# Two graph layers, one instruction order: a sum moves ahead of the output's statistics, the output's scaling moves back, and the first two periods are reordered

## The chip, the cores and the metric

The kernel runs on one core of a Trainium2 chip. Its time is the device time of one execution in microseconds (us); the figure given is the median of three runs. Five engines work side by side, each through its own list of instructions in order: TensorE (PE in the profile) multiplies, VectorE (DVE), ScalarE (ACT) and GpSimd (POOL) do the elementwise work, SyncE (SP) issues the transfers. They wait for each other through semaphores.

## The reference

There are 128 graphs of 128 nodes with 512 features. Each passes through two layers. The first is an attention over neighbours with 8 heads, the second a hypergraph convolution with a hidden width of 1024. Each layer is added to its input and normalized over the features.

```python
feats = einsum('bnf,hfu->bhnu', X, W)
dense = leaky_relu(e_self[..., :, None] + e_neigh[..., None, :], 0.2)
att   = softmax(dense + NEG_BIG * (1 - A), axis=-1)
x     = layernorm(x + relu(einsum('bhij,bhju->bhiu', att, feats) + b))

conv(x, W, b) = Dn * (H @ (Be * (H.T @ (x @ W.T)))) + b      # H = (adj != 0)
h     = layer_norm(relu(conv(x, W1, b1)), gamma, beta)
x     = layernorm(x + (conv(h, W2, b2) + x))
```

All of it is in fp32. A and H are the same 0/1 matrix of a graph, and H H^T with its two scalings is one 128 x 128 matrix, R in the kernel.

## The kernel before, in words

**Pairs.** Two graphs (g = 0, 1) make a pair, so there are 64 pairs (p). The three large products of a pair (features pf with W, hidden ph with W1, output weights py with W2) are each made as a 2 x 2 block product by seven smaller products instead of eight. The function `chain` lays down one such set. Its products go to three PSUM banks, called X, Y and W: 1 to X, 2 to Y, 6 onto X, 5 to W, 7 onto X, 4 onto X, 3 onto W, in this order. X is copied out by ACT (L343) after product 1, after product 6 and after product 7, and PE may add the next product to X only after that copy. The four quarters of the result are then sums of two pieces. For the hidden values h these sums are `h_sum` (L865, on DVE); `relu` (L880, on ACT) follows each of them. `h_sum(g, q)` makes quarter q of graph g; the one in question is `h_sum(1, 0)`, which needs products 1 and 6 and, last, 5 and 3 (bank W). For the features the sums are `f_sum` (L508 on DVE, one quarter on ACT). The sums of operands that the seven products need are made ahead: for the inputs xS, zS and hS on POOL, for the weights once at the start (`prepare_hidden` for W1, L248; `prepare_output_blocks` and `prepare_output_block_sums` for W2, L299 and L225).

**The order is written out by hand.** Each operation of a pair is registered with `at(lag, time, ...)` or `@step(lag, time)`: a lag in periods and a time within a period of T = 38.6. Its key is time + (p + lag) * T. All operations of all pairs are sorted by their keys once and emitted in this order, and each engine runs its own share in that order. The keys are places in a row, not real times. So in one period of the steady state the kernel works on several pairs at once: loads and masks of pair p, features of p - 1, attention of p - 2, hidden layer of p - 3, output of p - 4. The table `first` overrides keys for the first pairs, and `todo` holds the work done once, with keys of its own; there the first full period begins at 115.8.

**PE's order in a period**: `propagate` (pz, R times the first layer's output y), `propagator` (pd, makes R for a later pair), ph products 1, 2, 6, 5, 7, `output` (pq, R times y2), ph products 4 and 3, pf products 1, 2, 6, 5, 7, py product 1, pf products 4 and 3, the attention `attend_pair` (pav), py products 6, 2, 7, 5, 4, 3.

**DVE's order around the change**: `o_sum` for both graphs (L1023, adds the output to the skip path), `o_stats` for both (bn_stats L758 and bn_aggr L759), the variance column of `rstds` (L764), `h_sum(1, 0)` (L865), the transposes eT of graph 0's attention (L639), `o_norm` (L769, scales the output), `f_sum` twice (L508), eT of graph 1, the last `f_sum`, and `spread_rows` (rows, L541).

**POOL**: the power of `rstds` (L766 gives rso for the output and rsa for the first layer), `squares` (L903, sums squares of h in three levels for each graph), `h_sums` (hS, L468), then the mask of a pair (neg, L377), rsa, `masked` (L588, adds the mask to the neighbour scores nb), zS (L839), and others.

**ACT**: copies of X (L343), relu, the squares of h (L891), the first layer's output (L793), zT (`z_evict`, L828: pz out of PSUM), `leaky` (L604) and `exponential` (L618) on nb. `largest` (L610, on DVE) stands between these two.

**Transfers.** All go through SP's queue in the order of the keys: e_write and e_read (ed, eb: the attention scores to DRAM and back), `load_blocks` (xb), `store` (L1041, 512 KB of output), `load_edges` (ab), then rows are written to DRAM (rd, L551) and read back spread over all partitions as nb (L569, two transfers of 512 KB). `load` brings a (adjacency) and w; w has one buffer, which `nodes` (L359 to L368) reads.

Of the kernel before, what the change touches and what calls it, by code (L numbers as in the profile page):

```python
# [20 lines left out]
def kernel(  # L21
# [45 lines left out]
    nc = tc.nc  # L67
# [244 lines left out]
    LAST = PAIRS - 1  # L312
    steps = []

    def step(lag, time, since=0, until=PAIRS):

        def keep(fn):
            steps.append((lag, time, fn.__name__, range(since, until), fn, ()))
            return fn
        return keep  # L320

    def at(lag, time, fn, *args, since=0, until=PAIRS):
        steps.append((lag, time, fn.__name__, range(since, until), fn, args))
# [444 lines left out]
    def normalize(s, key, t, g):  # L768
        nc.vector.tensor_scalar(  # L769
            t, t, s["mv", key][:, g, 0:1], s["rs", key][:, g:g + 1], op0=ALU.subtract,  # L770
            op1=ALU.mult,
        )
# [95 lines left out]

    at(3, 5.9, h_sum, 0, 0, 0, "Y")
    at(3, 10.75, h_sum, 1, 1, 2, "W")  # L870
    at(3, 16.4, h_sum, 1, 0, 1, "W")

    def relu(p, s, g, q):
        dst = hid(s, g, q)
# [44 lines left out]
    def weigh(s, i, to, start):  # L919
# [3 lines left out]
          QU, 1, until=LAST)  # L923
# [105 lines left out]
    at(4, 13.3, o_sum, 1, until=LAST)  # L1029
    at(4, 14.7, o_stats, 0, until=LAST)  # L1030
    at(4, 15.5, o_stats, 1, until=LAST)
    at(4, 15.6, rstds, "o", until=LAST)

    @step(4, 17.0, until=LAST)
    def o_norm(p, s):
        for g in range(2):
            normalize(s, "o", s["o"][:, g, :], g)

    @step(4, 19.5, until=LAST)
    def store(p, s):  # L1040
        nc.sync.dma_start(out[2 * p:2 * p + 2].rearrange("g n f -> n g f"), s["o"])  # L1041

# [79 lines left out]
    for t, fn, *args in (  # L1122
# [20 lines left out]
        (12.95, load_first_row, (1,)),  # L1143
        (15.46, load_weights, (nc.sync, w1_blocks[:1:-1], w1t, F // 2, HALF)),
        (16.1, everywhere, (b2_bc, b2, nc.sync)),
        (79.0, prepare_hidden, (nc.gpsimd, 2)), (79.1, prepare_hidden, (nc.gpsimd, 0)),
        (98.0, prepare_hidden, (nc.gpsimd, 1)), (110.6, prepare_hidden, (nc.vector, 3)),
        (15.5, prepare_output_vectors, ()), (16.0, prepare_output, ()),
        (78.3, prepare_rows, ()), (78.79, prepare_output_sums, ()),
        (78.99, prepare_output_spread, (0, "gw")), (98.0, prepare_output_spread, (1, "bw")),  # L1150
# [2 lines left out]
        (117.8, prepare_output_blocks, (slice(2, 3),)),  # L1153
        (118.1, prepare_output_blocks, (slice(3, 4),)),
        (126.5, prepare_output_block_sums, (nc.gpsimd, slice(0, 2))),
        (127.7, prepare_output_block_sums, (nc.vector, slice(2, 3))),
        (134.5, prepare_output_block_sums, (nc.vector, slice(3, 4))),
        (100.0, prepare_mean_columns, ()),
    ]

# [5 lines left out]
        ("r_evict", 0): 97.845,  # L1166
        ("spread_rows", 1): 15.72, ("nodes", 1): 15.55, ("write_nodes", 1): 15.85,
        ("edges", 1): 110.4, ("scale_edges", 1): 110.5, ("neighbours", 1): 80.1,
        ("propagator", 1): 117.76, ("spread_nodes", 1): 80.3, ("r_evict", 1): 121.8,
        ("leaky", 0, 1, 1): 77.65, ("leaky", 0, 0, 1): 73.6, ("largest", 0, 0, 1): 75.3,  # L1170
        ("attend", 0, 0, 0): 78.95, ("attend", 0, 0, 1): 78.96, ("attend", 0, 1, 0): 78.97,
        ("attend", 0, 1, 1): 78.98, ("attended", 0, 0): 97.8, ("attended", 0, 1): 97.82,
        ("add_bias", 0, 0): 13.6, ("add_bias", 0, 1): 13.61,
        ("residual", 0, 0): 97.81, ("residual", 0, 1): 97.83, ("rstds", 0, "a"): 97.84,
        ("leaky", 1, 0, 0): 117.85, ("leaky", 1, 0, 1): 117.9, ("leaky", 1, 1, 0): 119.9,
        ("largest", 1, 0, 0): 118.0, ("largest", 1, 0, 1): 118.2, ("largest", 1, 1, 0): 120.2,
        ("masked", 1, 0, 0): 109.0, ("masked", 1, 1, 1): 121.5,
        ("nodes", 2): 142.2, ("write_nodes", 2): 143.0, ("nodes", 3): 150.0,
        ("write_nodes", 3): 150.1, ("skip", 0): 132.5,
    }  # L1180

    def run(fn, p, args):
# [87 lines left out]
```

## Time and profile before

| | |
|---|---|
| time, median of 3 runs | 2442.08 us (2441.72 to 2445.27) |
| span of the profiled execution | 2440.8 us |
| PE busy | 2369.9 us (97%) |
| DVE busy | 2000.1 us (82%) |
| POOL busy | 1816.2 us (74%) |
| ACT busy | 1524.7 us (62%) |
| DMA, mean rate | 142 GB/s |

The span is that of one traced execution. Busy time is the time in which an engine has at least one instruction under way; for PE the ends are modelled. A line of a timeline gives start, duration, engine, line of the kernel, operation, what is written and read, shapes and how often in a row; in brackets stands the engine's idle time just before and what ended it. A line of waits gives who waited for whom: total us, how often, the longest. The core ran at a mean granted clock of 0.998.

### The profile page before, as it was taken

What the parts mean: (1) busy time and instruction counts of PE and PEld (TensorE: products, weight loads), DVE (VectorE), ACT (ScalarE), POOL (GpSimd) and SP (SyncE); (2) the same over time, 40 slices, a digit from 0 to 9 for tenths busy, and PEclk for the clock granted to TensorE, in tenths of its full rate; (3) what the DMA queues carried; (4) which work ended last, traced back from release to release, by engine and by line L of the source; (5) the groups of instructions that cost most, each with busy time, mean ns of one, the idle gap of its engine ahead of it and who ended that gap; (6) DMA issues with size and microseconds to landing.
All of it is one profiled execution on the core that took longest, in us unless ns stands there. A gap on an engine that the chain in (4) does not pass through costs nothing.

```text
span 2440.8 us, 81033 instructions
## 1 busy us (share of the span) xinstructions
PE 2369.9 (97%) x32309; PEld 2009.1 (82%) x32309; DVE 2000.1 (82%) x4456; ACT 1524.7 (62%) x4481; POOL 1816.2 (74%) x2060
## 2 busy tenths in 40 slices
PE   7999999999999999999999999999999999999998
PEld 5788888888888888888888888888888888888886
DVE  7888878888887888888888888887887888888876
ACT  4665756756656657557666566575576665665663
POOL 5777777777777777777777777777777777777774
PEclk9999999999999999999999999999999999999999
DMA  6545455545555455454445554544554555545441
GB/s 185 139 132 154 141 137 145 150 142 145 147 145 147 133 151 146 137 148 145 141 147 146 145 147 137 149 145 141 148 146 138 147 145 146 147 135 154 140 122 53
DMA packets 432872, 347.10 MB, mean 142 GB/s; under 512 B 153176, under 2 KB 382064, under 8 KB 432496
## 3 DMA queue, kind: packets, MB, share of 16 engines
q1 hardware_dynamic: 429024, 337.46, 48.4%
q8 instruction: 255, 4.18, 0.7%
q10 hardware_dynamic: 3472, 4.47, 0.6%
q14 instruction: 121, 0.99, 0.1%
HBM read 239.08 MB, written 102.73 MB: 140 GB/s over the span
## 4 chain that ended last, share of the span: by engine, by line
PE 83%; DVE 6%; ACT 5%; DMA 2%; issue 2%; POOL 1%; SPq 0%; ACTq 0%; POOLq 0%; DVEq 0%
PE pyX L97 17%; PE phX L97 16%; PE pyW L97 8%; PE phW L97 7%; PE pfX L97 7%; PE phY L97 4%; PE pav L702 4%; PE pz L97 4%; PE pyY L97 4%; PE pq L97 4%; ACT h L880 3%; PE pfW L97 2%; DVE h L865 2%; PE pfY L97 2%; PE pd L97 1%
## 5 line engine op out<-in xcount | busy, mean ns | idle before, releaser
L343 ACT COPY py<-pyX 128x257 f32<-128x257 f32 x189 | 70.9, 375 | 511.0 <-PE pyX L97 511.0
L97 PEld LDWEIGHTS phX<-zS,w_sb 128*64 128x64 f32 x6144 | 350.3, 137 | 38.1 <-POOL ft L741 23.1
L97 PE MATMUL phX<-zS,w_sb 128*64 128x128 f32 x6144 | 373.0, 273 | 4.3 <-POOL xS L468 2.2
L903 POOL TENSOR_TENSOR sq<-sq 128x512 f32<-128x512 f32 (+2 forms) x384 | 349.6, 911 | 20.1
L588 POOL TENSOR_TENSOR nb<-nb,neg 128x512 f32<-128x512 f32 x256 | 319.6, 1281 | 37.6 <-DMA nb<-rd 37.1
L604 ACT ACTIVATE nb<-nb,ft 128x128 f32<-128x128 f32 x1020 | 325.3, 392 | 19.2 <-POOL nb L588 17.3
L618 ACT ACTIVATE nb<-nb,nm 128x128 f32<-128x128 f32 x1024 | 319.1, 391 | 4.0 <-DVE nm L610 4.0
L880 ACT ACTIVATE h<-h,vecs 128x128 f32<-128x128 f32 x768 | 239.5, 393 | 76.7 <-DVE h L865 76.4
L766 POOL TENSOR_TENSOR rso<-veo,mhalf 128x2 f32<-128x2 f32 x63 | 44.2, 702 | 292.5 <-DVE veo L764 292.5
L97 PE MATMUL pyX<-w_sb,hS 128*64 128x257 f32 x2016 | 243.7, 379 | 0.5 <-POOL hS L468 0.5
L97 PE MATMUL pyX<-w_sb,h 128*64 128x257 f32 x2016 | 243.5, 379 | 0.5 <-ACT py L343 0.5
L97 PE MATMUL pyW<-w_sb,hS 128*64 128x256 f32 x2016 | 242.9, 378 | 0.4 <-DVE y L934 0.4
L97 PEld LDWEIGHTS pyX<-w_sb,h 128*64 128x64 f32 x2016 | 172.1, 136 | 47.7 <-ACT py L343 0.9
L97 PEld LDWEIGHTS pyW<-w_sb,hS 128*64 128x64 f32 x2016 | 171.5, 136 | 47.2 <-POOL neg L377 0.8
L741 POOL TENSOR_TENSOR ft<-ft,b_bc 128x512 f32<-128x512 f32 x128 | 203.9, 1613 | 6.4 <-ACT ft L532 6.4
L610 DVE TENSOR_REDUCE nm<-nb 128x4 f32<-128x512 f32 x256 | 175.3, 685 | 34.1 <-ACT nb L604 32.2
L97 PEld LDWEIGHTS pyX<-w_sb,hS 128*64 128x64 f32 x2016 | 165.5, 137 | 41.1 <-POOL hS L468 0.7
L97 PE MATMUL pfX<-w_sb,xS 128*64 128x264 f32 x992 | 136.2, 390 | 40.3 <-ACT pf L343 40.1
L639 DVE STREAM_TRANSPOSE eT<-eb 128x512 f32<-128x512 f32 x252 | 163.5, 687 | 0.0
L1006 DVE SCALAR_TENSOR_TENSOR y<-y,rsh,bw_bc 128x512 f32<-128x512 f32 x126 | 150.5, 1233 | 14.3 <-POOL rsh L1002 14.3
L804 DVE SCALAR_TENSOR_TENSOR o<-y,b_bc 128x512 f32<-128x512 f32 x128 | 162.1, 1305 | 0.0
L891 ACT ACTIVATE sq<-h 128x512 f32<-128x512 f32 x256 | 160.8, 629 | 2.1
(178 smaller groups left out, 5567.9 us busy)
## 6 DMA issues: line engine op xcount, KB each, us to landing
nb<-rd SPq DMA_DIRECT2D x127, 512.0 KB
ed<-nb SPq DMA_DIRECT2D x126, 512.0 KB
eb<-ed SPq DMA_DIRECT2D x504, 128.0 KB
x<-in_x_dram SPq DMA_DIRECT2D x64, 512.0 KB
out_dram<-o SPq DMA_DIRECT2D x63, 512.0 KB
xb<-in_x_dram SPq DMA_DIRECT2D x248, 128.0 KB
a<-in_adj_dram SPq DMA_DIRECT2D x64, 128.0 KB
w<-in_adj_dram SPq DMA_DIRECT2D x128, 64.0 KB
```

The lines of the kernel that those rows point to most:

```text
L97: nc.tensor.matmul(to[rows], lhs[:, rows], rhs, start=start, stop=stop, skip_group_check=True)
L588: nc.gpsimd.tensor_tensor(t, t, neg[:, :, None, :].to_broadcast([P, NB, HH, B]), op=ALU.add)
L604: nc.scalar.activation(t, t, AF.Prelu, bias=s["ft"][:, g, h, 0:1], alpha=SLOPE)
L610: nc.vector.tensor_reduce(s["nm"][:, g, hs], scores(p, s, g, hs).rearrange("p b h j -> p h b j"), AX.XY, ALU.max, negate=True,)
L618: nc.scalar.activation(t, t, AF.Exp, bias=s["nm"][:, g, h:h + 1])
L639: nc.vector.transpose(s["eT"][:, g, hs, :].rearrange("p h (b i) -> p h b i", b=NB), s["eb", g][:, :, hs, :].rearrange("p b h j -> p h b j"),)
L741: nc.gpsimd.tensor_tensor(t, t, b0_bc.rearrange("p (h u) -> p h u", h=H), op=ALU.add)
L804: nc.vector.scalar_tensor_tensor(s["o"][:, g, :], s["y"][:, g, :], 2.0, b2_bc, op0=ALU.mult, op1=ALU.add)
L880: nc.scalar.activation(dst[:, k, :], src[:, k, :], AF.Relu, bias=b1_sb[:, c:c + 1])
L891: nc.scalar.activation(s["sq"][:, g, q * KH // 2:(q + 1) * KH // 2, :], hid(s, g, q), AF.Square, scale=DH ** -0.5,)
L903: nc.gpsimd.tensor_tensor(t[:, :n, :], t[:, :n, :], t[:, n:2 * n, :], op=ALU.add)
L1006: nc.vector.scalar_tensor_tensor(t, t, s["rs", "h"][:, g:g + 1], bw_bc.rearrange("p (j c) -> p j c", j=2), op0=ALU.mult, op1=ALU.add,)
```

## The change

No instruction is added or taken away; keys change. It is meant to let each engine reach sooner what PE needs next.

In the steady state, `h_sum(1, 0)` goes ahead of the output's statistics in DVE's order (key 14.6, between `o_sum` at 13.3 and `o_stats` at 14.7). The columns for the output's scale are made later (17.3), behind `squares` of graph 0 on POOL and behind eT of graph 0 on DVE. `o_norm` moves behind eT of graph 1 (23.0), and the store behind `load_blocks` and `load_edges`, right ahead of the write of rows (24.3).

In the first two periods, the sums of W1 are made in the order in which the products use them; `masked`, `leaky` and `largest` of pair 1 come earlier, `propagator` of pair 1 later; two exponentials of pair 1 go behind the copies of X that stood behind them; `prepare_output_block_sums` on DVE, `squares` of pair 0 and `nodes` of pairs 2 and 3 with their transfers go later.

```diff
-    at(3, 16.4, h_sum, 1, 0, 1, "W")
+    at(3, 14.6, h_sum, 1, 0, 1, "W")
...
-    at(4, 15.6, rstds, "o", until=LAST)
-
-    @step(4, 17.0, until=LAST)
+    at(4, 17.3, rstds, "o", until=LAST)
+
+    @step(4, 23.0, until=LAST)
     def o_norm(p, s):
...
-    @step(4, 19.5, until=LAST)
+    @step(4, 24.3, until=LAST)
     def store(p, s):
...
-        (79.0, prepare_hidden, (nc.gpsimd, 2)), (79.1, prepare_hidden, (nc.gpsimd, 0)),
-        (98.0, prepare_hidden, (nc.gpsimd, 1)), (110.6, prepare_hidden, (nc.vector, 3)),
+        (79.0, prepare_hidden, (nc.gpsimd, 0)), (79.1, prepare_hidden, (nc.gpsimd, 1)),
+        (120.7, prepare_hidden, (nc.gpsimd, 2)), (110.6, prepare_hidden, (nc.vector, 3)),
...
-        (127.7, prepare_output_block_sums, (nc.vector, slice(2, 3))),
-        (134.5, prepare_output_block_sums, (nc.vector, slice(3, 4))),
+        (137.5, prepare_output_block_sums, (nc.vector, slice(2, 3))),
+        (141.0, prepare_output_block_sums, (nc.vector, slice(3, 4))),
...
-        ("propagator", 1): 117.76, ("spread_nodes", 1): 80.3, ("r_evict", 1): 121.8,
+        ("propagator", 1): 121.7, ("spread_nodes", 1): 80.3, ("r_evict", 1): 121.8,
...
-        ("leaky", 1, 0, 0): 117.85, ("leaky", 1, 0, 1): 117.9, ("leaky", 1, 1, 0): 119.9,
-        ("largest", 1, 0, 0): 118.0, ("largest", 1, 0, 1): 118.2, ("largest", 1, 1, 0): 120.2,
-        ("masked", 1, 0, 0): 109.0, ("masked", 1, 1, 1): 121.5,
-        ("nodes", 2): 142.2, ("write_nodes", 2): 143.0, ("nodes", 3): 150.0,
-        ("write_nodes", 3): 150.1, ("skip", 0): 132.5,
+        ("leaky", 1, 0, 0): 113.0, ("leaky", 1, 0, 1): 117.9, ("leaky", 1, 1, 0): 119.9,
+        ("largest", 1, 0, 0): 110.55, ("largest", 1, 0, 1): 118.2, ("largest", 1, 1, 0): 120.2,
+        ("masked", 1, 0, 0): 98.0, ("masked", 1, 0, 1): 98.1, ("masked", 1, 1, 0): 98.2, ("masked", 1, 1, 1): 121.5,
+        ("exponential", 1, 0, 0): 119.85, ("exponential", 1, 1, 1): 126.6,
+        ("squares", 0, 0, 0): 141.3, ("squares", 0, 0, 1): 141.4, ("squares", 0, 0, 2): 141.5,
+        ("nodes", 2): 144.2, ("write_nodes", 2): 144.3, ("spread_nodes", 2): 145.5,
+        ("nodes", 3): 154.6, ("write_nodes", 3): 154.7, ("skip", 0): 132.5,
```

## The prediction

> **What bounds the kernel now.** I read the page's busy times first: TensorE (PE) is the only engine near its limit.
>
> ```profile
> PE 2369.9 (97%) x32309; PEld 2009.1 (82%) x32309; DVE 2000.1 (82%) x4456; ACT 1524.7 (62%) x4481; POOL 1816.2 (74%) x2060
> ```
>
> So only a change of PE's own pauses counts. The list of PE's waits is second: one recurring line carries nearly all of it, the rest is the start.
>
> ```profile
> PE pfX L97 <- ACT pf L343: 40.1, 60, 1.0
> PE px L396 <- DMA x<-in_x_dram: 8.7, 1, 8.7
> ```
>
> Third, the timeline of one period, engine by engine. PE: after product 5 (pfW), product 7 (pfX) waits for ScalarE's (ACT's) copy of product 6 out of the same bank.
>
> ```profile
> 1009.56 1.09 PE L97 MATMUL pfX<-w_sb,xS 128*64 128x264 f32 x8
> 1010.45 1.09 PE L97 MATMUL pfW<-w_sb,xS 128*64 128x264 f32 x8
> 1012.17 1.11 PE L97 MATMUL pfX<-w_sb,xS 128*64 128x264 f32 x8 [0.64 <-ACT pf L343]
> 1013.08 1.94 PE L97 MATMUL pyX<-w_sb,h 128*64 128x257 f32 x16
> ```
>
> ACT: that copy stands behind the relu of h's second graph, first half (L880), which waits 1.21 for VectorE (DVE).
>
> ```profile
> 1008.90 0.38 ACT L343 COPY pf<-pfX 128x264 f32<-128x264 f32 x1 [0.48 <-PE pfX L97]
> 1010.48 1.28 ACT L880 ACTIVATE h<-h,vecs 128x128 f32<-128x128 f32 x4 [1.21 <-DVE h L865]
> 1011.67 0.36 ACT L343 COPY pf<-pfX 128x264 f32<-128x264 f32 x1
> ```
>
> DVE: the sum that relu needs (L865) stands behind both output statistics.
>
> ```profile
> 1006.80 1.24 DVE L1023 TENSOR_TENSOR o<-o,pq 128x512 f32<-128x512 f32 x2
> 1007.96 0.68 DVE L758 BATCH_NORM_STATS2 statso<-o 128x6 f32<-128x512 f32 x1
> ...
> 1009.69 0.17 DVE L764 TENSOR_SCALAR veo<-mvo 128x2 f32<-128x2 f32 x1
> 1009.77 0.68 DVE L865 TENSOR_TENSOR h<-ph,phW 128x512 f32<-128x512 f32 x1
> ...
> 1011.59 1.45 DVE L769 TENSOR_SCALAR o<-o,mvo,rso 128x512 f32<-128x512 f32 x2
> ...
> 1016.83 0.43 DVE L508 TENSOR_TENSOR ft<-pf,pfW 128x264 f32<-128x264 f32 x1 [1.46 <-PE pfW L97]
> ```
>
> A control exists: in the last period with pf products DVE has no "nodes" work, its sum comes 1.2 us earlier, and PE does not pause.
>
> ```profile
> 2350.83 1.09 PE L97 MATMUL pfX<-w_sb,xS 128*64 128x264 f32 x8
> 2351.72 1.09 PE L97 MATMUL pfW<-w_sb,xS 128*64 128x264 f32 x8
> 2352.61 1.09 PE L97 MATMUL pfX<-w_sb,xS 128*64 128x264 f32 x8
> ```
>
> **What the Trainium skill says.** "PSUM — Partial Sum Buffer", section "Engine vs sequencer instructions": the queues of ScalarE, VectorE and GpSimd are strict FIFO. The trace agrees: the copy at 1011.67 had its data from 1010.65 and went only after the relu. "Perfetto Trace Analysis", section "Tensor Engine Instruction (MATMUL, LD_WEIGHTS)": a matmul's end is modelled, so I count start to start: 1.72 from pfW to pfX here, 0.89 in the control; the pause costs 0.83, not 0.64. "DMA: Bandwidth & Descriptors", section "Queues, rings and completion order": each DMA engine takes the descriptors of one ring in ring order. That matters for the moved store, and no run here yet shows a small write directly behind it.
>
> **The change part by part.**
>
> *h_sum(1,0) to 14.6.* It moves between o_sum and o_stats; no instruction is added. Its input phW (started 1006.03, 1.94 long) ends at 1007.97, when DVE finishes o_sum (1008.04), so the new wait in front of the statistics is under 0.1. Sum 1008.0 to 1008.7; the relu follows ACT's first copy at 1009.2, ends 1010.4; product 6 is ready at 1010.65, its copy runs to 1011.03, product 7 may start at its natural 1011.34. Slack 0.3. The gain is 0.83, plus 0.02 at the next product, which starts 0.91 instead of 0.89 later. The periods agree: pz to pz is 37.24 in the steady state (1028.87 to 1066.11) and 36.37 in the control (2332.92 to 2369.29), 0.87 apart. Between 0.85 and 0.87 I take 0.86: 60 x 0.86 = 51.6.
>
> *o_stats, rstds, o_norm, store.* Behind the statistics on DVE stand eT, the pf sums and rows; they keep their order but for o_norm. DVE's new order from 1008.7: statistics 1.73, eT 1.22, veo 0.08, pf sum 0.35; then the pf sum that waits for product 7's copy (1011.34 + 1.56 = 1012.90), 0.34; eT 1.22; o_norm 1.37; end 1015.85. The next pf sum is ready at 1016.83 - 0.86 = 1015.97. o_norm fits into the old idle time of 1.46, with 0.1 to spare, and costs nothing. On GpSimd (POOL) the power for rso now stands behind the squares of graph 0, which need no DVE, so hS starts about 0.8 earlier than now: hidden.
>
> *The store* is the risk. Now:
>
> ```profile
> 1013.07 0.41 SPq L1041 DMA_DIRECT2D out_dram<-o  x1
> 1013.52 3.00 SPq L137 DMA_DIRECT2D ab<-in_adj_dram  x4
> 1017.64 0.34 SPq L551 DMA_DIRECT2D rd<-rows  x1
> 1019.08 1.51 SPq L569 DMA_DIRECT2D nb<-rd  x2
> ```
>
> New: o_norm's end 1015.9, store issued then, rd issued at 1017.64 - 0.86 = 1016.8. The 512 KB store now moves about 0.9 to 2.5 after issue (DMA is busiest from 1014 to 1015.5), so until about 1018.4; rd's write would land at 1018.2 and lands 0.65 later if it queues (0 if it does not, 1.5 if the store is slow). Then nb, masked on POOL, leaky on ACT, zT, phX are 0.65 late against PE. How much is free? POOL waited 2.61 for nb at 280.43, ACT then 2.00, and PE lost 0.81: PE loses what POOL's wait has over 1.8. POOL's usual wait is 37.1 / 39 = 0.95, so 0.85 is free. Only periods that are already late lose: three before. I allow 2.0 in all.
>
> *The first two periods.* The keys only change order; each instruction stays. Three edits follow one thought: POOL makes the weights' sums in the order of the products (0 and 1 early, 2 only ahead of product 7), masked, leaky and largest of pair 1 go ahead into ACT's and POOL's idle time before pz (ACT waits 1.36 there at 50.15, a leaky group takes 1.28), and no exponential stands ahead of a copy that PE needs. PE's pauses between 48 and 101 now: the propagator ahead of product 1 (phX starts 53.76 though zT is there at 50.74), 1.8 for ph's first copy behind an exponential that waits for DVE, 2.2 at 66.83 for the third copy behind the last exponential, 1.4 at 97.22. New: product 1 at 51.9, the first copy at 53.9 without the wait, product 6 at 55.3, propagator behind it. Then DVE, which is busy without a gap from 46 to 65 and does the same work, holds PE: its last block of prepare_output_blocks frees the bank of phW at 58.9, largest gives the exponential ahead of the second copy at 59.6, so product 7 is at 61.4 (now 62.72), product 4 at 64.4 (now 66.83), pfX at 67.9 (now 70.34). In the pf stretch the block sums move off DVE's path to f_sum and the squares behind hS on POOL, so rows leave near 77.5 (now 80.26). pz(1) then waits for a(3), which is loaded behind nb: rsa about 2.5 to 3 earlier than 91.33. Gain kept: 3.0, bounds 0 (the wait for a is unmoved) and 5.
>
> Sum: 2442.1 - 51.6 - 3.0 + 2.0 = 2389.5.
>
> **The rivals.**
>
> *The store takes the place of the copy.* If rd is 2.0 late instead of 0.65, each of the 39 periods in which POOL waits loses 0.95 + 2.0 - 1.8 = 1.15: 45 in place of the 2.0 allowed, so about 2432. For it: rd, nb, masked is a chain of 8 us with 0.85 free. Against: rd is only 16 KB and the store 512 KB, over in 1.5 us.
>
> *A rest of the wait stays.* If DVE reaches the sum 0.5 later than worked out (TENSOR_SCALAR beside a busy POOL varies: deg took 1.18 at 1028.09 where two columns elsewhere take 0.17), the copy is 0.25 late: 60 x 0.25 = 15, about 2405.
>
> *Slower.* The sum blocks DVE, and rows and rd come late with the store ahead: nb 2.4 later costs 0.95 + 2.4 - 1.8 = 1.55 in 39 periods, 60 in all, so about 2447. Against: phW ends before DVE is free, and the control shows 36.37 is reachable.
>
> **How the numbers follow.** Forecast 0.74, a rest of the wait 0.12, the store 0.09, slower or no gain 0.05. The time is the forecast's, 2389.5. Low 2382: no loss at nb, 5 at the start, and the three old pauses of zT (1.2) gone. High 2408: the rest of the wait. Faster by over 0.2% 0.94, same 0.03, slower 0.03.
>
> **What would show it.** Right: PE's line for pfX on pf gone, pfW to pfX 0.89, pz to pz near 36.4, sum L865 ahead of L758, o_norm ending within 0.2 of the last pf sum's start. The start: pz of pair 1 near 90.5 (now 93.44). Store: nb issued 2.1 to 2.8 after rd instead of 1.44, POOL's wait for nb grown from 37.1 to some 70. Wrong: a large PE line phX on zT or pq on y, a period above 36.8, or o_norm holding the last pf sum and rows.

## The result, and the profile after

The changed kernel takes 2464.82 us (median of 4 runs, 2460.85 to 2468.28) against 2442.34 of the kernel before (2441.72 to 2445.27; a fourth run stands beside the three above): ratio 1.0089 (1.0070 to 1.0108). It is 0.9% slower. The forecast was 2389.5, faster by 52.7; it was wrong, and the rival that forecast a slower kernel came nearest.

First the busy times, then the engines of the chain that ended last, on the page of the changed kernel; the last line is the chain of the kernel before:

```profile
PE 2378.2 (96%) x32309; PEld 1899.6 (77%) x32309; DVE 2040.1 (83%) x4456; ACT 1527.6 (62%) x4481; POOL 1807.7 (73%) x2060
...
PE 37%; DMA 28%; DVE 14%; POOL 8%; ACT 7%; SPq 3%; issue 3%; DVEq 0%; ACTq 0%; POOLq 0%
```

```profile
PE 83%; DVE 6%; ACT 5%; DMA 2%; issue 2%; POOL 1%; SPq 0%; ACTq 0%; POOLq 0%; DVEq 0%
```

PE is still the busiest engine, but it makes up only 37% of the chain, 83% before. 28% is DMA, 2% before. The list of PE's waits (who waited for whom: total us, times, longest) names the new wait:

```profile
PE phX L97 <- ACT zT L828: 53.7, 48, 2.6
PE px L396 <- DMA x<-in_x_dram: 8.0, 1, 8.0
PE pyW L97 <- DVE y L934: 5.0, 8, 1.0
PE pyX L97 <- POOL hS L468: 4.2, 2, 2.8
```

The line for pfX on pf, 40.1 before, is gone. In its place stands phX on zT. The list of all waits shows where that comes from (the last line shown is the first one's in the kernel before; there the second had 17.3 in 17 waits, and SP's wait for rd 79.4):

```profile
POOL nb L588 <- DMA nb<-rd: 129.5, 67, 6.2
...
ACT nb L604 <- POOL nb L588: 83.5, 55, 8.0
```

```profile
SPq L569 <- DMA rd<-rows: 163.0, 63, 4.1
```

```profile
POOL nb L588 <- DMA nb<-rd: 37.1, 39, 5.3
```

So nb comes late, POOL's masked is late, ACT's leaky is late, and zT stands behind leaky on ACT. The wait is there at the transfer rd already.

Start to start, PE's excess over the shortest time of each pair of products, summed from pair 1's pz on, makes the balance. Before: pfW to pfX 51.9, all else 7.1. After: pfW to pfX 0.2; pd to phX 61.5; phX and phY that run slowly after such a pause 9.6; pyX to pyW 6.0; pav to pyX 3.3; all else 3.6. That is 25 more, and 1.1 gained ahead of it (pz of pair 1 starts at 92.30 instead of 93.44). The last pair's pz starts 24.2 later than before (2424.83 against 2400.67).

One period of the changed kernel, DVE first:

```profile
1660.59 1.24 DVE L1023 TENSOR_TENSOR o<-o,pq 128x512 f32<-128x512 f32 x2
1661.75 0.68 DVE L865 TENSOR_TENSOR h<-ph,phW 128x512 f32<-128x512 f32 x1
1662.35 0.69 DVE L758 BATCH_NORM_STATS2 statso<-o 128x6 f32<-128x512 f32 x1
...
1666.83 1.30 DVE L639 STREAM_TRANSPOSE eT<-eb 128x512 f32<-128x512 f32 x2
1668.06 2.31 DVE L769 TENSOR_SCALAR o<-o,mvo,rso 128x512 f32<-128x512 f32 x2
1670.29 0.41 DVE L508 TENSOR_TENSOR ft<-pf,pfW 128x264 f32<-128x264 f32 x1
1670.81 0.24 DVE L541 STREAM_TRANSPOSE rows<-ft 128x32 f32<-128x32 f32 x1
```

The sum L865 follows o_sum at once, as predicted. But o_norm takes 2.31 for its two instructions, not 1.45, and the last pf sum, whose bank PE finished at about 1669.5, starts only at 1670.29. POOL at that time makes hS:

```profile
1666.15 2.51 POOL L468 TENSOR_TENSOR hS<-h 128x512 f32<-128x512 f32 x2
1668.74 1.34 POOL L468 TENSOR_TENSOR hS<-hS,h 128x512 f32<-128x512 f32 x1
1670.16 1.35 POOL L468 TENSOR_TENSOR hS<-h,hS 128x512 f32<-128x512 f32 x1
...
1679.82 4.98 POOL L588 TENSOR_TENSOR nb<-nb,neg 128x512 f32<-128x512 f32 x4 [1.69 <-DMA nb<-rd]
```

SP's queue, in this period and in an earlier one:

```profile
652.39 0.41 SPq L1041 DMA_DIRECT2D out_dram<-o  x1
653.07 0.34 SPq L551 DMA_DIRECT2D rd<-rows  x1
657.36 0.92 SPq L569 DMA_DIRECT2D nb<-rd  x2
...
1670.39 0.41 SPq L1041 DMA_DIRECT2D out_dram<-o  x1
1671.07 0.34 SPq L551 DMA_DIRECT2D rd<-rows  x1
1673.45 0.93 SPq L569 DMA_DIRECT2D nb<-rd  x2
```

From rd to nb it was 1.44 before. Here it is 2.38, and in the earlier period 4.29. Both periods have the store directly ahead of rd.

### The profile page after: what moved, and what is told of

Its sections match the earlier page's. It is cut to its first block, busy times and chain, and to the rows that moved or that the text cites. A ratio compares the mean times of both kernels' runs of the same rounds, so it can differ in the third digit from the quotient of the medians.

```text
span 2464.9 us, 81039 instructions
## 1 busy us (share of the span) xinstructions
PE 2378.2 (96%) x32309; PEld 1899.6 (77%) x32309; DVE 2040.1 (83%) x4456; ACT 1527.6 (62%) x4481; POOL 1807.7 (73%) x2060
## 4 chain that ended last, share of the span: by engine, by line
PE 37%; DMA 28%; DVE 14%; POOL 8%; ACT 7%; SPq 3%; issue 3%; DVEq 0%; ACTq 0%; POOLq 0%
PE phX L97 12%; DMA nb<-rd 11%; DMA rd<-rows 6%; PE phW L97 6%; DMA ed<-nb 5%; DVE o L769 5%; PE pfX L97 5%; ACT nb L604 4%; POOL nb L588 3%; PE phY L97 3%; DVE eT L639 3%; PE pq L97 3%; DMA eb<-ed 3%; PE pyX L97 2%; DMA sd<-sr 2%
## 5 line engine op out<-in xcount | busy, mean ns | idle before, releaser
L903 POOL TENSOR_TENSOR sq<-sq 128x512 f32<-128x512 f32 (+2 forms) x384 | 317.8, 828 | 215.4 <-ACT sq L891 195.3
L97 PEld LDWEIGHTS phX<-zS,w_sb 128*64 128x64 f32 x6144 | 344.9, 137 | 38.9 <-POOL ft L741 15.6
L97 PEld LDWEIGHTS pyW<-w_sb,hS 128*64 128x64 f32 x2016 | 149.2, 136 | 75.8 <-issue 6.8
L97 PEld LDWEIGHTS pyX<-w_sb,h 128*64 128x64 f32 x2016 | 149.3, 137 | 70.6 <-ACT py L343 0.9
L741 POOL TENSOR_TENSOR ft<-ft,b_bc 128x512 f32<-128x512 f32 x128 | 194.9, 1542 | 5.0 <-ACT ft L532 5.0
L97 PEld LDWEIGHTS pyX<-w_sb,hS 128*64 128x64 f32 x2016 | 144.6, 137 | 64.5 <-POOL hS L468 4.5
L97 PE MATMUL phX<-zT,w_sb 128*64 128x128 f32 x2048 | 131.0, 283 | 54.1 <-ACT zT L828 53.7
L639 DVE STREAM_TRANSPOSE eT<-eb 128x512 f32<-128x512 f32 x252 | 164.2, 690 | 13.4 <-DMA eb<-ed 13.3
L766 POOL TENSOR_TENSOR rsa<-vea,mhalf 128x2 f32<-128x2 f32 x64 | 44.8, 700 | 173.7 <-DVE vea L764 173.7
L97 PEld LDWEIGHTS phX<-zT,w_sb 128*64 128x64 f32 x2048 | 115.4, 141 | 67.5 <-ACT zT L828 67.1
L468 POOL TENSOR_TENSOR hS<-h 128x512 f32<-128x512 f32 x126 | 159.6, 1287 | 4.7 <-DVE w_sb L225 4.7
```

The costliest lines, as they stand in the source:

```text
L97: nc.tensor.matmul(to[rows], lhs[:, rows], rhs, start=start, stop=stop, skip_group_check=True)
L468: engine.tensor_tensor(t[:, i], in0, in1, op=op)
L639: nc.vector.transpose(s["eT"][:, g, hs, :].rearrange("p h (b i) -> p h b i", b=NB), s["eb", g][:, :, hs, :].rearrange("p b h j -> p h b j"),)
L741: nc.gpsimd.tensor_tensor(t, t, b0_bc.rearrange("p (h u) -> p h u", h=H), op=ALU.add)
L903: nc.gpsimd.tensor_tensor(t[:, :n, :], t[:, :n, :], t[:, n:2 * n, :], op=ALU.add)
```

## The experiments

Unless said otherwise each was timed in three rounds beside the kernel before on the same chip, and the ratio is to that kernel.

**The sum alone.** Theory: the early sum is worth what was forecast, and the late store and o_norm take it back. Rival: the early sum itself delays DVE.

```diff
-    at(3, 16.4, h_sum, 1, 0, 1, "W")
+    at(3, 14.6, h_sum, 1, 0, 1, "W")
```

> The kernel before with h_sum(1, 0) at 14.6 alone. Theory A (the scaling and the store moved back are the whole loss, the sum is the whole gain): pfW to pfX 0.89, period 36.4, rd to nb 1.45, about 2391 us (2442 less 60 x 0.86). Theory B (the sum ahead of the statistics itself delays DVE's later work, and nb with it): no gain or a loss, 2440 or more, with DVE's last pf sum later than PE's need.

2417.89 us, ratio 0.9886 (0.9869 to 0.9902). The sum alone is a gain, but of 28 and not of 51. The median period is 36.70, not 36.37. PE's list has a line that the forecast had not seen, and PE's timeline shows 2.13 from pav to pyX:

```profile
PE pyX L97 <- POOL hS L468: 3.0, 15, 0.3
```

```profile
1662.21 2.04 PE L702 MATMUL pav<-ft,eT 128*64 128x65 f32 x64
1664.34 1.96 PE L97 MATMUL pyX<-w_sb,hS 128*64 128x257 f32 x16
```

The list counts only 15 of these waits; the longer step is in every period. POOL's order explains it:

```profile
1657.04 0.70 POOL L766 TENSOR_TENSOR rso<-veo,mhalf 128x2 f32<-128x2 f32 x1 [5.27 <-DVE veo L764]
1657.70 2.74 POOL L903 TENSOR_TENSOR sq<-sq 128x512 f32<-128x512 f32 x3
1660.41 2.51 POOL L468 TENSOR_TENSOR hS<-h 128x512 f32<-128x512 f32 x2
1663.00 1.29 POOL L468 TENSOR_TENSOR hS<-hS,h 128x512 f32<-128x512 f32 x1
```

POOL idles 5.27 for the variance, which the sum has pushed back by its 0.6. Behind rso stand the squares and hS; the wait for the variance hands its delay down to hS. In the changed kernel rso stands behind the squares, and this pause is not there. That part of the change is good.

**The output's statistics, o_norm and the store put back, first two periods kept.** This tells what the reorder of the start is worth.

```diff
-    at(4, 17.3, rstds, "o", until=LAST)
+    at(4, 15.6, rstds, "o", until=LAST)
...
-    @step(4, 23.0, until=LAST)
+    @step(4, 17.0, until=LAST)
...
-    @step(4, 24.3, until=LAST)
+    @step(4, 19.5, until=LAST)
```

> The changed kernel with rstds, o_norm and store back at 15.6, 17.0 and 19.5, the rest of the change kept. Theory A: about 2390, within 3 of the run with the sum alone, so the new order of the first two periods is worth 0 to 3. Theory B: about 2465. Theory C (the first two periods' order upsets the later ones): 2400 or more while the sum alone is near 2391.

2417.95 us, ratio 0.9884 (0.9870 to 0.9899): the same as the sum alone. The reorder of the first two periods has no effect that these runs can tell from nothing. The 2.05% between this ratio and the changed kernel's, 50 us, come from the late rso, o_norm and store.

**The store away from rd**, o_norm still late: the changed kernel with the store behind the transfers that follow nb.

```diff
-    @step(4, 24.3, until=LAST)
+    @step(4, 32.0, until=LAST)
```

> The changed kernel with only the store moved on, from 24.3 to 32.0, behind the reads of the sums, so that it is no longer ahead of rd; o_norm stays late. If the store ahead of rd is the larger part of the loss (rd to nb 2.4 to 4.5 in place of 1.45): rd to nb back at 1.45, rows still 0.65 late, about 2395 to 2405. If the late o_norm beside hS on POOL is the larger part: 2430 or more with rd to nb at 1.45.

2439.69 us over 12 runs, ratio 0.9974 (0.9964 to 0.9983). So 28 of the 50 (1.0089 less 0.9974) are the store's place in this schedule. Neither of the two cases expected is met: the parts are near halves. From rd to nb it is 1.44 again in the median of periods 28 to 61. The other 22 stay with the late o_norm, and with the store now beside other transfers; PE's list has three smaller waits in place of the large one:

```profile
PE phX L97 <- ACT zT L828: 17.3, 23, 2.0
PE pav L702 <- DVE eT L639: 13.6, 14, 1.6
...
PE pyW L97 <- DVE y L934: 7.2, 19, 0.8
```

Some of the 22 belongs to the store's new place too. DVE's transposes eT now wait for the transfer eb, 50.6 in all where the changed kernel has 13.3 in 17 waits:

```profile
DVE eT L639 <- DMA eb<-ed: 50.6, 38, 2.9
```

```profile
1717.49 1.30 DVE L639 STREAM_TRANSPOSE eT<-eb 128x512 f32<-128x512 f32 x2 [0.43 <-DMA eb<-ed]
1718.72 3.01 DVE L769 TENSOR_SCALAR o<-o,mvo,rso 128x512 f32<-128x512 f32 x2
```

Here o_norm starts 0.43 later, right ahead of the next hS sum (1718.77), and takes 3.01; rd is issued 9.84 before pz, not 10.57. In 25 of the periods 10 to 61 rd is as late as that. Why eb comes late was not followed; the store is all that was moved.

**The late rso, o_norm and store without the sum**: the kernel before with only these three keys of the change.

```diff
-    at(4, 15.6, rstds, "o", until=LAST)
+    at(4, 17.3, rstds, "o", until=LAST)
...
-    @step(4, 17.0, until=LAST)
+    @step(4, 23.0, until=LAST)
...
-    @step(4, 19.5, until=LAST)
+    @step(4, 24.3, until=LAST)
```

> The kernel before with rstds, o_norm and store at 17.3, 23.0 and 24.3 alone; the sum stays at 16.4. Theory A, with parts that add: 2442 + 75 = about 2515, the pause of pfX on pf still there. If the parts do not add, because PE's pause for the copy gives the late store time back (rows and rd wait for the same last pf sum, which comes 0.86 later while the store does not): about 2450 to 2480. Theory B: no loss, 2442.

2534.49 us, ratio 1.0355 (1.0334 to 1.0376): 88 slower. PE has both waits, the old and the new:

```profile
PE phX L97 <- ACT zT L828: 65.1, 48, 2.7
PE pfX L97 <- ACT pf L343: 38.5, 54, 1.2
```

The sum is what takes away the one, the late output is what makes the other. Their times don't add: the sum alone gains 1.1% and these keys alone lose 3.6%, and together they lose 0.9%, some 38 us less than the sum of the two. All three expectations were missed. PE's steps account for most of the 38: the pause for hS, 19.6 over the run with the sum alone, goes away with the late rso; and without the sum o_norm takes 2.72 in the median, not 2.31, rd is issued 10.15 before pz, not 10.57, and the steps from pd to phX lose 75.5, not 61.5.

**o_norm and store in the middle**: the changed kernel with o_norm between the first two pf sums. The thought was that a fast DVE reaches o_norm early enough, and the store is gone before rd.

```diff
-    @step(4, 23.0, until=LAST)
+    @step(4, 18.3, until=LAST)
...
-    @step(4, 24.3, until=LAST)
+    @step(4, 21.0, until=LAST)
```

> The changed kernel with o_norm at 18.3 (behind the first pf sum, ahead of the second) instead of 23.0 and the store at 21.0 (behind load_edges, well ahead of rd) instead of 24.3; rstds stays at 17.3, behind the squares. The run with the sum alone kept a pause of 0.29 per period for hS, because rso stands ahead of the squares on POOL and waits for the statistics that the sum has pushed back. Theory A: with rso behind the squares hS is in time, rows and rd are in time, period 36.4: about 2395 to 2402. Rival: o_norm beside hS on POOL takes 2.3 instead of 1.45 wherever it stands, rows come late again, and the time stays at 2415 or more.

2477.68 us, ratio 1.0123 (1.0105 to 1.0140). The theory failed. The rival had the time and a long o_norm right, but not the way: rows and nb were in time (rd 11.44 before pz, 1.45 from rd to nb). The median period is 37.61. PE's wait and DVE's timeline:

```profile
PE pfW L97 <- DVE ft L508: 55.5, 61, 1.5
```

```profile
1661.12 0.42 DVE L508 TENSOR_TENSOR ft<-pf,pfY 128x264 f32<-128x264 f32 x1
1662.02 2.91 DVE L769 TENSOR_SCALAR o<-o,mvo,rso 128x512 f32<-128x512 f32 x2 [0.48 <-POOL rso L766]
1664.85 0.42 DVE L508 TENSOR_TENSOR ft<-pf,pfW 128x264 f32<-128x264 f32 x1
```

o_norm waits for rso, then takes 2.91 beside hS, and the pf sum behind it, which frees bank W for PE's product 3, is late. Here o_norm's own length is the cost: it is 1.45, 1.94, 2.31 and 2.91 in different places, with the same two instructions.

**Instruction fetches.** In the packets of the trace, rd's last 8 of 128 packets come late in periods 10 to 27 of the changed kernel (counted by the pair whose pz they precede). They start when a 16 KB packet of another queue ends: in period 17 that packet runs from 8.46 to 7.39 before pz, and the eight start at 7.39 before pz. The Trainium skill, "Runtime: NRT & Kernel Launch", section "Instruction fetch mechanics", says that each engine fetches its instructions in blocks of 16 KiB, 256 instructions, over a queue of its own. That would be these packets: the trace has 256 of them, and PE has 1021 instructions to a period in the trace, four blocks. The test adds 64 tiny products to PE at the start, whose results nothing uses; it was run once.

> The changed kernel with 64 tiny matmuls added on PE in its idle time at the start, whose results nobody uses: they move the places in PE's list where its instructions are fetched in 16 KB blocks by 128 instructions, some 4 us of PE's time. Theory (the fetch sits on one DMA engine just when rd's packets reach it, 8.5 to 7.4 us ahead of pz in periods 10 to 27, and makes rd to nb 4.3 instead of 2.4): the long waits for rd leave periods 10 to 27 and stand in other periods. Rival (the early periods are slow for another reason): rd to nb stays at 4.3 in periods 10 to 27.

2480.38 us; rd to nb stayed as it was and so did the packet. But the page counts 258 instructions more, one whole block and two, and the trace has 257 of these packets, so the test could hardly move anything. It was made again with half of it, 32 products and 129 instructions (`range(4)` for `range(8)`):

```diff
+    def fill_queue():
+        for b in range(4):
+            t = bank(f"fill_{b}")
+            for _ in range(8):
+                nc.tensor.matmul(t[:2, :64], ident[:, :2], ident[:, :64], start=True, stop=True)
```

> The changed kernel with 32 tiny products on PE at the start, whose results nothing uses; with their weight loads 129 more instructions. The earlier run with 64 added 259 instructions; 256 fetch packets of 16 KB serve the whole program, about four to a period of PE's some 1020 instructions, so 259 may have been one whole fetch and have left the fetches in place. Theory: the fetches are PE's own and their place is PE's instruction count; shifted by half a fetch, the packet that ended at -8.5 to -7.5 relative to pz in periods 10 to 27 stands some 4.6 away, rd to nb there falls from 4.2 to 4.5 to about 2.4, and later periods (35 to 61), where the packet had drifted away, show 4 and more. Rival: the fetches are not PE's, and the list stays as in the changed kernel.

The packet moved, from 8.5 ahead of pz to some 12.4 in periods 14 to 17, and the late periods moved with it. Time from rd to nb, median of the periods (us):

| kernel | 1 to 9 | 10 to 27 | 28 to 52 | 53 to 61 |
|---|---|---|---|---|
| before | 2.71 | 1.44 | 1.44 | 1.47 |
| changed | 3.20 | 4.26 | 2.38 | 2.35 |
| changed, +258 instructions | 3.31 | 4.24 | 2.38 | 2.33 |
| changed, +129 instructions | 2.36 | 2.37 | 2.97 | 4.23 |
| store away from rd | 2.19 | 2.79 | 1.44 | 1.44 |

So the fetches are PE's own, their place in a period is set by PE's instruction count, and one that lies across rd costs nearly 1.9 on top of the store. A near miss costs nothing: in period 29 of the changed kernel the fetch runs from 8.47 to 7.59 before pz, but rd's last packet has started at 8.67, and rd to nb is 2.38. The time did not fall (2482.50, one run), since other periods took the place of those freed: this was a test of the cause and no cure.

**hS ahead of the squares.** With the sum alone, hS was 0.3 late. This puts the squares of graph 0 behind hS on POOL.

```diff
-            at(3, ((17.0, 17.1, 17.2), (26.0, 27.3, 28.0))[g][level], squares, g, level)
+            at(3, ((24.0, 24.1, 24.2), (26.0, 27.3, 28.0))[g][level], squares, g, level)
```

> The kernel before with h_sum(1,0) ahead of the statistics, and on POOL the three squares of graph 0 (2.75 together) behind hS. Theory: the pause of 0.3 per period that stayed in the run with the sum alone (PE's product py 6 waiting for hS) comes from hS standing behind the power for rso and those squares; with 2.75 taken out ahead of hS it is gone, the steady period is 36.37 to 36.45 instead of 36.70, and the time is 2396 to 2402. Rival: hS is held by its input h (relu of graph 1, first half), then the pause and 2418 stay; or the squares behind hS delay the mask and rsa, then PE waits for zT or pz for rsa and the period is above 36.6.

2428.58 us, ratio 0.9931 (0.9916 to 0.9945), 11 above the sum alone. hS was early, and its line gone from PE's waits, yet the median period rose to 36.81. Both theory and rivals missed. DVE and PE show why:

```profile
1664.68 2.49 DVE L769 TENSOR_SCALAR o<-o,mvo,rso 128x512 f32<-128x512 f32 x2
1667.09 0.41 DVE L508 TENSOR_TENSOR ft<-pf,pfY 128x264 f32<-128x264 f32 x1
1667.43 0.42 DVE L508 TENSOR_TENSOR ft<-pf,pfW 128x264 f32<-128x264 f32 x1
```

```profile
1666.88 1.09 PE L97 MATMUL pfX<-w_sb,xT 128*64 128x264 f32 x8
1667.99 1.11 PE L97 MATMUL pfW<-w_sb,xS 128*64 128x264 f32 x8
1668.90 2.27 PE L702 MATMUL pav<-ft,eT 128*64 128x65 f32 x64
```

o_norm now runs beside hS and takes 2.49 instead of 1.94. The pf sum behind it frees bank W 0.6 later against PE's product 4 than in the best version below, product 3 starts 1.11 after product 4 instead of 0.89, and pav, which reads the last pf sum, is 0.2 longer.

**The store alone late**, o_norm early: the run just told with the store directly ahead of rd in the order.

```diff
-    @step(4, 19.5, until=LAST)
+    @step(4, 24.3, until=LAST)
```

> The run with hS first, and besides only the store moved to its late place, right ahead of rd; o_norm stays early. Theory (the store's place and the late o_norm each cost, and together more than their sum since both use the one slack of about 0.85 that masked has): rd to nb grows from 1.44 to about 2.4 but rows are on time, so nb is about 0.95 later, barely past the slack: 5 to 15 us above the run with hS first, more if the instruction fetch catches rd's last packets in some periods. Rival, the late o_norm alone is the cause: no difference to the run with hS first. Rival, the store's place alone is the cause: 30 us or more above it.

2432.84 us, ratio 0.9948 (0.9932 to 0.9965), which overlaps that of the run with hS first; the median period is the same 36.81, and rd to nb is 1.44 in the median of periods 10 to 52. o was ready so early that the store left 0.5 to 2.7 ahead of rd and was mostly through. That is the number of the first rival, but not its cause, since with o_norm late the store's place is worth 28. What stands of the theory is that the parts need each other: the late key of the store costs next to nothing here by itself, and much when o_norm is late too, because then the store leaves 0.68 ahead of rd.

**Only the third level of the squares behind hS** (0.52 instead of 2.75), on the kernel before with the sum:

```diff
+            at(3, ((17.0, 17.1, 24.2), (26.0, 27.3, 28.0))[g][level], squares, g, level)
```

> The kernel before with h_sum(1,0) ahead of the statistics, and only the third level of graph 0's squares (about 0.6) behind hS. Theory: the 0.3 by which hS is late in the run with the sum alone is covered by 0.6, and o_norm still runs mostly beside the squares and not beside hS, so that the sum of pf behind it frees its bank in time: steady period 36.37 to 36.45, 2396 to 2404. Rival: o_norm is slow beside any pair of POOL's (hS started 0.6 earlier meets it) and the pause on pf's bank of the run with hS first (0.15 each) takes its place: 2415 or more.

2406.10 us, ratio 0.9837 (0.9820 to 0.9853): the fastest version found, 1.6% faster than the kernel before. The time is 2 above the expected range (the traced run, the fastest of the four, took 2401.02), but the median period is 36.37, as in the forecast's control. The step from pav to pyX is 1.87 instead of 2.13:

```profile
1647.39 1.07 PE L97 MATMUL pfX<-w_sb,xT 128*64 128x264 f32 x8
1648.28 1.07 PE L97 MATMUL pfW<-w_sb,xS 128*64 128x264 f32 x8
1649.17 2.05 PE L702 MATMUL pav<-ft,eT 128*64 128x65 f32 x64
1651.04 1.93 PE L97 MATMUL pyX<-w_sb,hS 128*64 128x257 f32 x16
```

What it has over the forecast lies at the start, which is as before, and in its periods 2 to 9 and its last fourteen, where the period is up to 37.6 and rd to nb goes to 3.4; the packets show a fetch near rd there too.

**The second and the third level behind hS.**

> The same with the second and third level (about 1.5) behind hS. Theory: hS is early enough by far, but it meets half of o_norm: o_norm's two take 2.0 to 2.3 instead of 1.94, the pause on pf's bank is between 0 and 0.15, 2398 to 2412. Rival: no pause at all, 2396 to 2402, or as the run with hS first, 2428.

2433.02 us, ratio 0.9947 (0.9931 to 0.9964), as the run with hS first; the expected 2398 to 2412 was missed. o_norm's two take 2.49 again: its second instruction now starts beside an hS sum of 512 elements, where before it started beside the squares' second level of 256.

## Why the prediction was wrong

**The pause on pf's copy** was read rightly. The early sum waits for nothing, the relu goes right behind ACT's copy, pfW to pfX is 0.89 and the line is gone. The shortest periods of the changed kernel, with zT in time, are 36.37 to 36.39 long, as forecast. The gain of 0.86 a period is real; the last run but one keeps it over most of its length.

**The step that failed** is the pair "o_stats, rstds, o_norm, store" and "The store". It put o_norm at no cost, the queue at 0.65 and the loss of both at 2.0; they came to this.

1. "o_norm 1.37; end 1015.85 ... fits into the old idle time of 1.46, with 0.1 to spare, and costs nothing." It took 2.31, because its new place lies beside hS. The last pf sum and rows are 0.65 later: rd is issued 10.6 before pz, not 11.24. I took the duration from a place where half of it lay beside something else, and left 0.1 of room.
2. "rd's write would land at 1018.2 and lands 0.65 later if it queues". It queues, and lands 0.95 later: rd to nb is 2.38 instead of 1.44. In the packets of period 45 the store's run from 10.35 to 8.83 before pz and rd's from 8.99 on. That agrees with the ring order that the prediction cites from the Trainium skill, "DMA: Bandwidth & Descriptors", section "Queues, rings and completion order"; the packets don't name their DMA engine. Where PE's fetch lies across rd's last packets, in 17 of the 18 periods from 10 to 27, it is 2.8 later; this was not in the sum at all.
3. "Only periods that are already late lose: three before. I allow 2.0 in all." The loss is 61.5 in 56 periods (33 of it in periods 10 to 27, 20 in 28 to 61), and 9.6 more as PE restarts slowly. nb leaves 1.6 later than before in most of the later periods (0.65 and 0.95), and 3.5 later in periods 10 to 27. How much is free was measured on the wrong thing. PE loses nothing while masked starts 2.36 or more before pz, and else exactly what is missing: in 45 of the 46 late periods from 10 to 61 the lead of masked and PE's loss add up to 2.35 to 2.38. In the kernel before the lead was 3.91 in the median, so 1.55 were free and not 0.85 (37.1 / 39 counts only the periods in which POOL waits). In the changed kernel the lead is 1.46, and PE loses 0.9 in the median. Counted in POOL's wait the limit is not fixed: rsa, ahead of masked, ends 3.52 before pz instead of 4.17, so PE now loses what POOL waits over 1.15 (1.69 cost 0.53, 2.29 cost 1.14) and not over 1.8.

**The rivals.** The rival "slower" gave 2447 with nb 2.4 later and named the cause, rows and rd late with the store ahead. The mean delay is near it, an estimated 2.2 (18 periods of 3.5 and 43 of 1.6), and 5 of 100 was far too little for it. What I set against it, that the store is over in 1.5, was no argument: rd leaves 0.68 behind the store, so most of that 1.5 is ahead of it. Against the late rows I had only the 0.1.

**The signs.** Three signs of being wrong came: a large line phX on zT (53.7), a median period above 36.8 (37.47), and o_norm holding the last pf sum. The sign of being right, "o_norm ending within 0.2 of the last pf sum's start", came as well (1670.37 and 1670.29), because the sum waited for o_norm: it could not tell the two cases apart.

**The sums.** The low end of 2382 is 2384.3 by its own terms (2442.1 - 51.6 - 5.0 - 1.2), and a sum 0.5 later, with 0.3 of slack, makes the copy 0.2 late and not 0.25. Neither touches the outcome.

**The start.** Forecast 3.0; from pz of pair 0 to phX of pair 1 it went from 49.09 to 48.13, so 1.0. Product 1 of pair 0 starts at 52.17, not 51.9, but at half speed (3.68 instead of 1.95), after 2.02 of waiting for zT; and a wait of 2.84 for hS at 81.13 stands in front of pz of pair 1. The second run says that nothing of it reaches the end.

**A second thing not foreseen** is that the sum alone is worth 28 and not 51, since hS sits behind the statistics through rso on POOL. The changed kernel avoids this by its late rso, and pays for it with o_norm.

**What stays open.** In the run with the store away, 22 us are still lost. Its trace shows three waits, on zT, eT and y, and a late eb; how much of the 22 is the late o_norm alone, and how much the store's new neighbours, was not taken apart.

## What to carry to other kernels

An instruction moved in one engine's order also gets new neighbours on the other engines, here GpSimd beside VectorE: take its duration from the place where it will stand, and if no trace shows it there, give it the length of what runs beside it. Ask of every large transfer that is moved what small one is queued behind it and who waits for that; the spare time, here about 1.5, is used once, and two delays of 0.65 and 0.95 that each look harmless use it up together, before the fetch adds to them. Measure that spare time from what the last engine needs, not from how long one in between waits. When a pause is taken away, look for the next thing that hangs on the delayed instruction through another engine, here hS through rso: moving 0.5 us of POOL's work out of each period's way gave 12 us that the sum alone had left.

## What the runs showed of the hardware

**A tensor_scalar of VectorE beside GpSimd ends 0.28 after GpSimd's instruction.** In the thirteen traces, 1607 of the o_norm instructions (128x512) began while POOL had 0.19 or more of an elementwise instruction left, and all of them end 0.28 after that one ends (0.276 to 0.309), whatever their start: the duration is what POOL has left, plus 0.28. The 20 that began in the last 0.19 of one took 0.50 to 0.51, which is the length without a wait. In the run with o_norm in the middle, each of the two started with an hS sum and took 1.49. The Trainium skill, "SBUF — State Buffer", section "Who interferes with whom", says that such an instruction in its two-port mode and one of GpSimd exclude each other for a whole instruction, whichever is first. The trace agrees, and adds the price: up to 1.0 for an instruction of 0.5.

**Some pauses of PE of about 2 us halved its clock.** Before phX in one period of the changed kernel, PE idles 2.38; the product takes 3.61 instead of 1.92. The windows of its first part and of the time after it, with the granted clock as the third number from the end, show 0.50 and 1.00:

```profile
1240.20:1243.40 3.20, 3.20 (x31) 3.20 (x33) 1.04 (x5) 2.72 (x9) 3.12 (x7) 0.50 0.17 46
1244.00:1247.00 3.00, 3.00 (x60) 3.00 (x58) 1.38 (x3) 1.56 (x5) 2.84 (x5) 1.00 0.37 103
```

In the changed kernel pauses up to 2.07 before the same product left it at 1.97, and all four from 2.29 to 2.56 slowed it; their periods are 40.6 to 40.8 long, about 1.7 more than the pause itself explains. That is no sharp limit: over all the traces, 17 of 33 such pauses of 1.94 to 2.67 were followed by a slow product and a granted clock below 0.9, and none of the 57 from 1.2 to 1.92 was. What decides between them is open.

**An instruction fetch is a transfer like others.** A packet of 16 KB takes 0.9 to 1.4. In period 17 the last 8 of rd's 128 packets, the share of one of the 16 DMA engines, start only as it ends, and the whole transfer waits for them. The Trainium skill, "Runtime: NRT & Kernel Launch", section "Instruction fetch mechanics", calls the cost of passing from one block to the next "mostly hidden", which is said of the engine that fetches; here it was nearly 1.9 for another transfer of 16 KB that others wait for.
